# Fewer instructions on one to four numbers per partition, and another instruction order, in a one-core cross-attention and quantized-FFN kernel

## The chip, the cores and the metric

The kernel runs on one core of a Trainium2 chip. The metric is the device time of one execution in microseconds, as a median over runs. A separate profiled execution gives the instruction trace that the tables below are read from. The core has five engines that run side by side, each through its own instruction queue in order: PE (TensorE, matmuls), DVE (VectorE), ACT (ScalarE), POOL (GpSimd) and SP (SyncE, which here only issues DMAs).

## The reference: what is computed

Eight batches, each an input `x` of 256 rows by 512 columns and a second input (`media`) of the same size. Cut to what matters:

```
xn    = layernorm(x)
theta = theta_w . media + theta_b          phi = phi_w . xn + phi_b       g = g_w . xn + g_b
p     = softmax(theta^T phi)               t   = p g
h     = relu((t - mean(t)) * rsqrt(var(t) + 1e-5) * gamma + beta)      # mean over the whole batch
x     = x + tanh(g_xattn) * (out_w h + out_b + media)

y     = layernorm(x)
f     = silu(bitlinear(y, w1)) * bitlinear(y, w2)                       # 512 -> 2048
x     = x + tanh(g_ffn) * bitlinear(f, w3)                              # 2048 -> 512
```

`bitlinear` normalizes its input by its root mean square, quantizes each row to 8-bit levels by the row's largest magnitude, and quantizes the weights to -1, 0 and 1 by their mean magnitude. In the kernel, the quantized values are held as small integers in 16 or 8 bits and multiplied on PE; the scales come back afterwards as one number per row.

## The kernel before

**Tiles.** A row of `x` is a partition, so a batch is two tiles of 128 x 512 (index `c`). Attention works on batch `b`; the FFN works on row tiles `i = 2b + c`, sixteen in all, each with four groups `j` of 512 columns of `w1` (`ug`) and of `w2` (`uu`). Every PSUM tile is one of eight banks.

**Operations and their names.** The builder makes a list `OPS` of labelled operations, `name:b` or `name:i`. The ones that matter here:

- Layer norm of `x` (L344-355): `nb`, `na` statistics on DVE; `nr` adds the epsilon, `np` raises to -1/2 on POOL, `nm` negates the mean, `nx` applies both and writes `xn`.
- Projections and scores: `jtheta`, `jphi`, `jg` and `sm` on PE, `htheta`, `hphi`, `hg` copy them out of PSUM; `sx` takes the row maximum on DVE, `se` the exponential on ACT; `pd`, `pr`, `ph`, `pl` divide and split; `av` multiplies on PE.
- Norm over the batch (L560-593): `tx` copies the result, `tb`, `ta`, `tw` per-partition statistics, `tm` sums over partitions by a matmul with ones, `tu` divides by 128, `td` forms mean squared minus mean of squares, `tr` flips the sign and adds the epsilon, `tp` raises to -1/2 on POOL; `hc`, `hs`, `hr`, `hl` apply it.
- Out-projection and residual: `om` on PE, `oa` on DVE adds it to `x` and leaves each row's sum.
- FFN input (L635-684): `im` turns the row sum into minus the mean, once for each `c`; `iq` squares on ACT, `ir` takes the maximum on DVE, `iv`, `ie`, `ip`, `ic` make the scale, `iz` quantizes, `it` transposes by DMA. `ia`, `ib` form the row's scale, `if0` and `if1` multiply it by `w1`'s and `w2`'s factor (`back`, columns 0 and 1), `ig` takes the reciprocal (column 2).
- FFN tile `i` (L686-764): `us` (Silu, ACT, scaled by `back` column 0), `um` (product, DVE), `qs` sum of squares, `qa` row maximum, `qf` a floor for it out of `back` column 2, `qm`, `qc` the quantizing scale; `qe` an epsilon term out of `back` column 2, `qr`, `qp`, `qb` the factor for the way back; `qz` quantizes, `qt` transposes by DMA.
- Down-projection: `dm` and `da` plainly, or for batches 2 to 6 a seven-product scheme for 2 x 2 blocks (`tS` sums, `tP` products, `tU` and `tA` additions).
- Weights: `wl` loads a 1 MB chunk, `ws` sums magnitudes, `wr` and `wq` quantize; `wf` makes the factor of `w1` and `w2`.

**What sets the order.** Nothing is scheduled at run time. `CFG["order"]` (L68) is a written-out list of all 1512 operations; they are emitted in that order, and each engine executes its share in sequence. `CFG["alt"]` says for the operations that can run on several engines which one does. A small operation is declared by `tiny` (L162), which offers DVE (`v`) and POOL (`p`). All DMAs go through SP in the listed order, so one whose buffer isn't free holds the ones behind it. Work tiles come from pools: 31 buffers of 2 KB per partition, 7 of 4 KB, 7 of 8 KB; the weight chunks and the FFN's `h` share the last kind.

The small operations have the form

```python
def tiny(label, fn):
    op(label, v=lambda: fn(V), p=lambda: fn(G))
...
tiny(f"qf:{i}", lambda e_: e_.tensor_scalar(fl(), back()[:, c, 2:3], Q_EPS * RMS_EPS**0.5, 1.0, ALU.mult, ALU.mult))
```

Of the kernel before, what the change touches and what calls it, by code (L numbers as in the profile page):

```python
# [19 lines left out]
P = 128  # L20
# [69 lines left out]
def flamingo_gated_block(  # L90
# [86 lines left out]
    ones, neg_half = c_("ones", [P, P]), c_("neg_half", [P, 2 * DC])

    fac = {n: (c_(f"{n}_max", [P, DC]), c_(f"{n}_sum", [P, 1]), c_(f"{n}_back", [P, 1]), c_(f"{n}_fwd", [P, 1])) for n in ("phi", "g")}
    half_w = {n: c_(f"{n}_half", [P, 2, DC, L], F16) for n in ("phi", "g")}  # L180
    theta_hi, theta_lo = c_("theta_whi", [P, DC, L], F32R), c_("theta_wlo", [P, DC, L], F32R)
    cols2 = c_("cols2", [P, 2])
    bias = {"theta": (lambda: cols2()[:, 0:1]), "phi": (lambda: cols2()[:, 1:2])}

    whole_x = [b for b in range(B) if b not in CFG["xsplit"]]
    whole_m = [b for b in range(B) if b not in CFG["msplit"]]
    assert set(whole_x) <= set(whole_m)
    keep = {"phi": False, "g": any(b not in CFG["p32"] for b in whole_x), "theta": any(b not in whole_x for b in whole_m)}
    scaled_t = {n: c_(f"{n}_sc", [P, DC, L]) if k else w_(f"{n}_sc", [P, 2 * DC, L]) for n, k in keep.items()}
# [19 lines left out]
    def constants():  # L209
        op("C:ones", lambda: V.memset(ones(), 1.0))  # L210
        op("C:half", lambda: V.memset(neg_half(), -0.5))
        if CFG["p32"] or CFG["rpe"]:
            op("C:id0", lambda: G.memset(ident(), 0.0))
            op(
                "C:id1",
                lambda: G.affine_select(
                    out=ident(), in_=ident(), compare_op=ALU.not_equal, fill=1.0, base=0, pattern=[[-1, P]], channel_multiplier=1
                ),
            )
        wps = ps_("warm")  # L220

        op("C:warm", lambda: [PE.matmul(wps()[:, 0:P], ones(), ones(), start=True, stop=True) for _ in range(CFG["warm"])])
        for n in ("theta", "phi", "g"):
            load_proj(n)
        op("Lc:0", lambda: nc.sync.dma_start(out=cols(), in_=columns))
        op("Lgam:0", lambda: nc.sync.dma_start(out=gam(), in_=ln_gamma))
        op("Lbet:0", lambda: nc.sync.dma_start(out=bet(), in_=ln_beta))
        op("Low:0", lambda: nc.sync.dma_start(out=ow(), in_=out_wT))
        op("C:tanh", lambda: S.activation(tg(), gates(), AF.Tanh))
        if CFG["rpe"]:  # L230
            tiny("C:gid", lambda e: e.tensor_scalar(gident(), ident(), tg()[:, 0:1], 1.0, ALU.mult, ALU.mult))

        tiny("C:ow", lambda e: e.tensor_scalar(ow(), ow(), tg()[:, 0:1], 1.0, ALU.mult, ALU.mult))
        op("C:owh", a=lambda: S.copy(ow_hi(), ow()), v=lambda: V.tensor_copy(ow_hi(), ow()))
        tiny("C:owl", lambda e: e.tensor_tensor(ow_lo(), ow(), ow_hi().bitcast(F32), ALU.subtract))
        tiny("C:ob", lambda e: e.tensor_scalar(ob(), ob(), tg()[:, 0:1], 1.0, ALU.mult, ALU.mult))

        for n in ("phi", "g"):
            mx, sm, back, fwd = fac[n]
            tot = ps_(f"{n}_tot")
            op(f"C:{n}max", lambda n=n, mx=mx: V.tensor_reduce(mx(), proj_w[n](), AX.X, ALU.max, apply_absolute_value=True))
            op(f"C:{n}sum", lambda mx=mx, sm=sm: V.tensor_reduce(sm(), mx(), AX.X, ALU.add))
            op(f"C:{n}tot", lambda sm=sm, tot=tot: PE.matmul(tot()[:, 0:1], ones(), sm(), start=True, stop=True))
            lim = 1e-30 if n == "phi" else 1e-2
            op(f"C:{n}back", lambda tot=tot, back=back, lim=lim: V.tensor_scalar(back(), tot()[:, 0:1], lim, 1.0 / G_SCALE, ALU.max, ALU.mult))
            op(f"C:{n}fwd", lambda back=back, fwd=fwd: V.reciprocal(fwd(), back()))
            tiny(f"C:{n}w", lambda e, n=n, fwd=fwd: e.tensor_scalar(scaled_w[n](), proj_w[n](), fwd(), 1.0, ALU.mult, ALU.mult))  # L250
            op(
                f"C:{n}h",
                a=lambda n=n: S.copy(half_w[n]()[:, 0], scaled_w[n]()),
                v=lambda n=n: V.tensor_copy(half_w[n]()[:, 0], scaled_w[n]()),
            )
            tiny(f"C:{n}l", lambda e, n=n: e.tensor_tensor(half_w[n]()[:, 1], scaled_w[n](), half_w[n]()[:, 0], ALU.subtract))
        pback, pfwd = fac["phi"][2:]
        tiny("C:tw", lambda e: e.tensor_scalar(scaled_w["theta"](), proj_w["theta"](), pback(), 1.0, ALU.mult, ALU.mult))
        tiny("C:tb", lambda e: e.tensor_scalar(cols2()[:, 0:1], col["theta"](), pback(), 1.0, ALU.mult, ALU.mult))
        tiny("C:pb", lambda e: e.tensor_scalar(cols2()[:, 1:2], col["phi"](), pfwd(), 1.0, ALU.mult, ALU.mult))  # L260
        op(
            "C:th",
            a=lambda: S.copy(theta_hi(), scaled_w["theta"]()),
            v=lambda: V.tensor_copy(theta_hi(), scaled_w["theta"]()),
        )
        tiny("C:tl", lambda e: e.tensor_tensor(theta_lo(), scaled_w["theta"](), theta_hi().bitcast(F32), ALU.subtract))
        tiny("C:gback2", lambda e: e.tensor_scalar(gback(), fac["g"][2](), 1.0 / P_SCALE, 1.0, ALU.mult, ALU.mult))
# [4 lines left out]
    def weights(n):  # L272
# [30 lines left out]
        if n < 2:  # L303
            op(f"wf:{n}", lambda: V.tensor_scalar(wfac()[:, n : n + 1], wmean()[:, n : n + 1], 1.0 / (127.0 * Q_UNIT), None, ALU.mult))
        else:
            op(f"wf:{n}", lambda: V.tensor_scalar(wmean()[:, 2:3], wmean()[:, 2:3], tg()[:, 1:2], None, ALU.mult))
# [22 lines left out]
    def attention(b):  # L329
        xt, med = xs[b], meds[b]  # L330
        xsp, msp, osp = b in CFG["xsplit"], b in CFG["msplit"], b in CFG["osplit"]
        s32, p32 = b in CFG["s32"], b in CFG["p32"]

        w32 = {
            "phi": proj_w["phi"],
            "theta": scaled_w["theta"] if xsp else proj_w["theta"],
            "g": proj_w["g"] if p32 else scaled_w["g"],
        }
        bias_b = bias if xsp else col

        mv, rstd, nmu = s_("mv", f"mv{b}", [P, DC, 2]), s_("rstd", f"rstd{b}", DC), s_("nmu", f"nmu{b}", DC)
        xn = [w_(f"xn{b}_{c}", [P, T]) for c in range(DC)]
        for c in range(DC):
            st = s_("bst", f"bst{b}_{c}", V.BN_STATS_DIM)  # L344
            op(f"nb{c}:{b}", lambda c=c, st=st: V.bn_stats(st(), xt[c]()))  # L345
            op(f"na{c}:{b}", lambda c=c, st=st: V.bn_aggr(mv()[:, c, :], st()))
        tiny(f"nr:{b}", lambda e: e.tensor_scalar(rstd(), mv()[:, :, 1], LN_EPS, 1.0, ALU.add, ALU.mult))
        op(f"np:{b}", lambda: G.tensor_tensor(rstd(), rstd(), neg_half()[:, :DC], ALU.pow))
        tiny(f"nm:{b}", lambda e: e.tensor_scalar(nmu(), mv()[:, :, 0], -1.0, 1.0, ALU.mult, ALU.mult))

        def norm(eng, c):
            return eng.tensor_scalar(xn[c](), xt[c](), nmu()[:, c : c + 1], rstd()[:, c : c + 1], ALU.add, ALU.mult)

# [240 lines left out]
        else:  # L594
# [4 lines left out]
                p=lambda: G.tensor_scalar(h(), h(), 3e38, 0.0, ALU.min, ALU.max),  # L599
            )  # L600

        osums = sums[b] = []
        for c in range(DC):
            o = ps_(f"o_ps{b}_{c}")

# [28 lines left out]
    def ffn_in(b):  # L634
# [10 lines left out]

        for c in range(DC):
            sq = w_(f"fsq{b}_{c}", [P, T])  # L650
            tiny(f"im{c}:{b}", lambda e, c=c: e.tensor_scalar(nmu()[:, c : c + 1], sums[b][c](), -1.0 / T, 1.0, ALU.mult, ALU.mult))  # L651
# [308 lines left out]
```

## Time and profile before

| what | value |
|---|---|
| median of 3 runs | 280.13 us (279.75 to 280.41) |
| profiled execution: device time | 279.37 us |
| profiled execution: span of the trace | 277.6 us |
| instructions on DVE, ACT, POOL | 537, 337, 273 |
| granted clock of PE | 0.999 |
| first real matmul | 6.47 us |
| last matmul ends | 274.38 us |

The profile's groups give, for each source line and shape, how many instructions ran, how long the engine was busy with them, the mean of one, and how long the engine had idled just before them. The timeline lists instructions by start, with the idle time before one and what ended it in brackets. The chain of waits goes back from the end: at each step to what released an instruction, or to its predecessor on the engine.

### The profile page before, as it was taken

How to read it: one execution, taken by the hardware profiler on the slowest of the kernel's cores; microseconds unless marked ns; L12 is line 12 of the kernel's file. 1: busy time of each engine (PE TensorE's matmuls, PEld its weight loads, DVE VectorE, ACT ScalarE, POOL GpSimd, SP SyncE). 2: the span in 40 equal slices, each digit the busy share in tenths (PEclk: the TensorE clock that was granted, in tenths of full speed). 3: DMA queues.
4: the chain of work that ended last, by engine and by line, in shares of the span. 5: the costliest groups of instructions: out<-in, count | busy, mean ns of one | idle time of the engine just before them, and what ended most of it. 6: DMA issues, size and time to landing. Idle time of an engine off the chain costs nothing.

```text
span 277.6 us, 4741 instructions
## 1 busy us (share of the span) xinstructions
PE 271.3 (98%) x1574; PEld 166.9 (60%) x1574; DVE 254.0 (91%) x537; ACT 227.6 (82%) x337; POOL 205.9 (74%) x273
## 2 busy tenths in 40 slices
PE   7999999999899999999999999999999999999995
PEld 7458585564365555545754778655545566457863
DVE  3798988999999989989999899997999889999895
ACT  1399999999989999899999899895867789675910
POOL 2588774799999998867896989758785855873461
PEclk9999999999999999999999999999999999999999
DMA  7999979998761325134948815916372356605685
GB/s 217 357 347 374 387 277 367 184 195 327 154 115 38 79 41 110 40 76 130 155 97 180 161 41 113 154 34 118 88 142 76 61 130 113 151 2 110 77 211 212
DMA packets 81528, 43.30 MB, mean 156 GB/s; under 512 B 67936, under 2 KB 69088, under 8 KB 81504
## 3 DMA queue, kind: packets, MB, share of 16 engines
q1 hardware_dynamic: 81504, 43.00, 62.2%
q8 instruction: 12, 0.20, 0.3%
q14 instruction: 12, 0.10, 0.1%
HBM read 22.02 MB, written 4.19 MB: 94 GB/s over the span
## 4 chain that ended last, share of the span: by engine, by line
PE 82%; DVE 8%; ACT 3%; issue 2%; DMA 2%; POOL 1%; SPq 0%; POOLq 0%; ACTq 0%
PE fup L699 18%; PE fgp L699 17%; PE dp L857 10%; PE fop L772 6%; PE av L538 4%; PE sc L463 4%; PE phi_ps L385 4%; PE theta_ps L385 3%; PE gx_ps L416 3%; PE tp L498 3%; PE o_ps L610 3%; PE sc L461 3%; PE av L551 3%; DVE nmax L472 2%; DMA med<-in_media 2%
## 5 line engine op out<-in xcount | busy, mean ns | idle before, releaser
L699 PEld LDWEIGHTS <-fqt 128*128 128x128 f16 x512 | 49.0, 99 | 56.8 <-issue 3.2
L699 PE MATMUL fgp<-w1q,fqt 128*128 128x512 f16 x256 | 61.7, 379 | 1.4 <-ACT fh L709 1.4
L699 PE MATMUL fup<-w2q,fqt 128*128 128x512 f16 x256 | 62.3, 379 | 0.0
L709 ACT ACTIVATE fh<-fgp,fback 128x512 f32<-128x512 f32 x64 | 41.1, 687 | 10.4 <-PE fgp L699 8.9
L711 DVE TENSOR_TENSOR fh<-fup,fh 128x512 f32<-128x512 f32 x64 | 42.6, 681 | 2.8 <-PE fup L699 1.6
L732 DVE TENSOR_REDUCE fham<-fh 128x1 f32<-128x2048 f32 x15 | 34.2, 2280 | 0.1
L731 ACT ACTIVATE fhq<-fh 128x2048 bf16<-128x2048 f32 x15 | 28.7, 1913 | 0.4 <-POOL fhfl L733 0.4
L745 ACT ACTIVATE fhq<-fh,fhqs 128x2048 f16<-128x2048 f32 (+1 forms) x14 | 26.6, 1907 | 1.9 <-DVE fhqs L735 1.7
L475 ACT ACTIVATE e<-sc,nmax 128x512 f32<-128x512 f32 x32 | 21.8, 689 | 2.8 <-DVE nmax L472 2.3
L772 PE MATMUL fop<-w3q,fhi 128*128 128x512 fp8e4 (+1 forms) x112 | 22.9, 349 | 0.0
L472 DVE TENSOR_REDUCE nmax<-sc 128x1 f32<-128x512 f32 x32 | 21.6, 681 | 0.7 <-PE sc L463 0.3
L450 POOL TENSOR_TENSOR x<-x,med 128x512 f32<-128x512 f32 x14 | 19.3, 1375 | 3.8 <-ACT med L444 3.7
L519 DVE SCALAR_TENSOR_TENSOR ph<-e,rden,ph 128x512 f16<-128x512 f32 x24 | 17.8, 760 | 0.0
L857 PEld LDWEIGHTS <-fhi 128*128 128x128 f16 x160 | 15.6, 98 | 3.6
L538 PE MATMUL av<-pt,gx 128*128 128x256 f16 x144 | 17.5, 273 | 0.0
L772 PEld LDWEIGHTS <-fhi 128*128 128x128 f16 x112 | 10.6, 98 | 9.3 <-DMA fhi<-fhq 0.4
L538 PEld LDWEIGHTS <-gx 128*128 128x128 f16 x144 | 13.8, 98 | 3.4 <-issue 0.3
L667 POOL TENSOR_SCALAR fq<-x,fnmu,fqs 128x512 f16<-128x512 f32 x16 | 14.1, 889 | 0.8 <-DVE fqs L663 0.2
L654 ACT ACTIVATE fsq<-x,fnmu 128x512 f32<-128x512 f32 x16 | 11.5, 719 | 3.1 <-DVE fnmu L651 2.3
L345 DVE BATCH_NORM_STATS2 bst<-x 128x6 f32<-128x512 f32 x16 | 10.8, 683 | 3.3 <-DMA x<-in_x 3.2
L416 PEld LDWEIGHTS <-xh 128*128 128x128 f16 x144 | 9.4, 98 | 5.5 <-issue 3.3
L621 DVE SCALAR_TENSOR_TENSOR x<-o_ps,x 128x512 f32<-128x512 f32 x16 | 10.9, 687 | 1.9 <-PE o_ps L610 1.6
(223 smaller groups left out, 688.9 us busy)
## 6 DMA issues: line engine op xcount, KB each, us to landing
x<-in_x SPq DMA_DIRECT2D x16, 256.0 KB, 4.0
med<-in_media SPq DMA_DIRECT2D x16, 256.0 KB, 4.5
w<-in_w2T SPq DMA_DIRECT2D x4, 1024.0 KB, 7.7
w<-in_w1T SPq DMA_DIRECT2D x4, 1024.0 KB, 8.2
w<-in_w3T SPq DMA_DIRECT2D x4, 1024.0 KB, 9.7
out<-x SPq DMA_DIRECT2D x15, 256.0 KB, 2.3
fhi<-fhq SPq DMA_TRANSPOSE x17, 4.4
gam<-in_ln_gamma SPq DMA_DIRECT2D x1, 256.0 KB, 10.4
```

The costliest lines, as they stand in the source:

```text
L385: PE.matmul(ps(), w, v, start=c == 0 and k == 0, stop=c == DC - 1 and k == e)
L472: op(f"sx{t}:{b}", lambda sc=sc, nmax=nmax: V.tensor_reduce(nmax(), sc(), AX.X, ALU.max, negate=True))
L475: lambda t=t, sc=sc, nmax=nmax, e=e: S.activation(e(), sc(), AF.Exp, bias=nmax(), accum_out=den()[:, t : t + 1]),
L538: PE.matmul(av()[:, ts(g, TG * P)], gx()[:, hg, ts(s, L)], v[:, hp, s], start=k == 0, stop=k == 3 * TCH - 1)
L699: PE.matmul(ps(), qt()[:, c * EC + k, :], wq[n][j]()[:, k, :], start=k == 0, stop=k == EC - 1)
L709: lambda j=j, gp=gp: S.activation(h()[:, ts(j, 512)], gp(), AF.Silu, scale=back()[:, c, 0:1]),
L711: op(f"um{j}:{i}", lambda j=j, up=up: V.tensor_tensor(h()[:, ts(j, 512)], up(), h()[:, ts(j, 512)], ALU.mult))
L731: op(f"qs:{i}", lambda: S.activation(hq().bitcast(BF16), h(), AF.Square, accum_out=ss()[:, 0:1]))
L732: op(f"qa:{i}", lambda: V.tensor_reduce(am()[:, 0:1], h(), AX.X, ALU.max, apply_absolute_value=True))
L745: return S.mul(hq()[:, sl], h()[:, sl], qs())
L772: PE.matmul(o()[:, sl], hi()[:, f, :], wq[2][f // 4]()[:, f % 4, sl], start=f == 0, stop=f == FC - 1)
L857: PE.matmul(banks[n]()[:, h * HT : (h + 1) * HT], l()[:, f, :], r(f), start=f == 0, stop=f == HC - 1)
```

## The change

54 instructions fewer (1512 operations become 1458): 64 go and 10 come.

- `nm` goes (8): `nx` subtracts the mean where it added the negated one.
- `tr` goes (8): the epsilon is added in `tu`, by a constant tile `eps2` with 0 and 1e-5, and `td` subtracts the other way round, so that `tp` can take its result. Two memsets (`C:e0`, `C:e1`) fill `eps2`.
- `im` is done once for both `c` (8 fewer); the two row sums now lie in one tile.
- `if0` and `if1` become one `if` that multiplies by both factors at once (8 fewer), with both inputs broadcast.
- `qf` goes (16): its constant is taken into `w2`'s factor in `wf`, so that the reciprocal in `back` column 2 is the floor.
- `qe` goes (16): a new `ge` (8, on DVE) writes the epsilon term for both `c` into `back` column 3.

Beside that, the lists of engines and of the order are replaced as a whole. Of the operations kept, 40 go from POOL to DVE, 39 from DVE to POOL, 11 from ACT to POOL, 12 from POOL to ACT, 9 from ACT to DVE and 3 from DVE to ACT. The matmuls are the same ones in another order, as are the 105 DMA issues. The order of the first DMAs, for example:

```
before  Lx0:0 Lx1:0 LWtheta Lm0:0 Lm1:0 Lc LWphi Lm0:1 Lx1:1 Lx0:1 Lx0:3 Lm1:1 LWg Low ... wl1:0 wl3:0 wl0:0 Lgam wl2:0 Lbet Lm0:3 wl0:2
after   Lx0:0 Lx1:0 Lm0:0 LWtheta Lm1:0 LWphi LWg Lc Lx0:1 Lx1:1 Lx0:2 Lx1:2 Low ... wl3:0 wl1:0 Lbet wl0:0 Lgam wl0:2 wl2:0 Lm1:5
```

and DVE's order from batch 0's residual sums to the factor that its first Silu reads:

```
before  oa1:0 oa0:0 hs:1 pl3:2 ir1:0 ir0:0 pl2:2 ie:0 ltheta:3 lphi:3 wm:0 lg:2 wn:0 wc:0 oa0:1 oa1:1 sx1:3 im1:1 sx0:3
        lg:3 sx2:3 wq2:0 wq3:0 sx3:3 wf:0 wf:1 ir0:1 ir1:1 wq2:1 iv:1 wq3:1 if0:0
after   oa0:0 oa1:0 hs:1 wm:0 pl2:2 ir1:0 ir0:0 wn:0 ie:0 wc:0 lg:2 lphi:3 ic:0 ltheta:3 lg:3 oa0:1 wq2:0 oa1:1 im:1 wq3:0
        sx2:3 wq0:1 sx0:3 sx3:3 ir0:1 ir1:1 iv:1 sx1:3 ia:0 ie:1 wf:0 ib:0 tb:2 wq2:1 if:0
```

The diff of the code, without the two long lists:

```diff
+    eps2 = c_("eps2", [P, 2])
+    op("C:e0", lambda: G.memset(eps2(), 0.0))
+    op("C:e1", lambda: G.memset(eps2()[:, 1:2], LN_EPS))
...
-            op(f"wf:{n}", ... wmean()[:, n : n + 1], 1.0 / (127.0 * Q_UNIT), None, ALU.mult)
+            unit = 1.0 / (127.0 * Q_UNIT) / (Q_EPS * RMS_EPS**0.5 if n else 1.0)
+            op(f"wf:{n}", ... wmean()[:, n : n + 1], unit, None, ALU.mult)
...
-        tiny(f"nm:{b}", lambda e: e.tensor_scalar(nmu(), mv()[:, :, 0], -1.0, 1.0, ALU.mult, ALU.mult))
-            return eng.tensor_scalar(xn[c](), xt[c](), nmu()[:, c : c + 1], rstd()[:, c : c + 1], ALU.add, ALU.mult)
+            return eng.tensor_scalar(xn[c](), xt[c](), mv()[:, c, 0:1], rstd()[:, c : c + 1], ALU.subtract, ALU.mult)
...
-        op(f"tu:{b}", lambda: V.tensor_scalar(mu(), mps()[:, 0:2], 1.0 / P, None, ALU.mult))
+        op(f"tu:{b}", lambda: V.scalar_tensor_tensor(mu(), mps()[:, 0:2], 1.0 / P, eps2(), ALU.mult, ALU.add))
-            lambda: V.scalar_tensor_tensor(var(), mu()[:, 0:1], mu()[:, 0:1], mu()[:, 1:2], ALU.mult, ALU.subtract),
+            lambda: V.scalar_tensor_tensor(
+                var(), mu()[:, 0:1], mu()[:, 0:1], mu()[:, 1:2], ALU.mult, ALU.subtract, reverse1=True
+            ),
-        tiny(f"tr:{b}", lambda e: e.tensor_scalar(rs(), var(), -1.0, LN_EPS, ALU.mult, ALU.add))
-        op(f"tp:{b}", lambda: G.tensor_tensor(rs(), rs(), neg_half()[:, 0:1], ALU.pow))
+        op(f"tp:{b}", lambda: G.tensor_tensor(rs(), var(), neg_half()[:, 0:1], ALU.pow))
...
+        tiny(f"im:{b}", lambda e: e.tensor_scalar(nmu(), sums[b](), -1.0 / T, 1.0, ALU.mult, ALU.mult))
-            tiny(f"im{c}:{b}", lambda e, c=c: e.tensor_scalar(nmu()[:, c : c + 1], sums[b][c](), -1.0 / T, 1.0, ALU.mult, ALU.mult))
...
-        for k in range(2):
-            tiny(f"if{k}:{b}", lambda e, k=k: e.tensor_scalar(back()[:, :, k], am(), wfac()[:, k : k + 1], 1.0, ALU.mult, ALU.mult))
+        tiny(f"if:{b}", lambda e: e.tensor_tensor(back()[:, :, 0:2], am().unsqueeze(2).to_broadcast([P, DC, 2]),
+                                                  wfac().unsqueeze(1).to_broadcast([P, DC, 2]), ALU.mult))
+        op(f"ge:{b}", lambda: V.scalar_tensor_tensor(back()[:, :, 3], back()[:, :, 2], 1.0 / Q_EPS**2, back()[:, :, 2], ALU.mult, ALU.mult))
...
-        tiny(f"qf:{i}", lambda e_: e_.tensor_scalar(fl(), back()[:, c, 2:3], Q_EPS * RMS_EPS**0.5, 1.0, ALU.mult, ALU.mult))
-        op(f"qm:{i}", lambda: V.tensor_scalar(am()[:, 0:1], am()[:, 0:1], fl(), 1.0 / (127.0 * Q_UNIT), ALU.max, ALU.mult))
+        op(f"qm:{i}", lambda: V.tensor_scalar(am()[:, 0:1], am()[:, 0:1], back()[:, c, 2:3], 1.0 / (127.0 * Q_UNIT), ALU.max, ALU.mult))
-        tiny(f"qe:{i}", lambda e_: e_.tensor_scalar(e(), back()[:, c, 2:3], back()[:, c, 2:3], RMS_EPS, ALU.mult, ALU.mult))
-        tiny(f"qr:{i}", lambda e_: e_.tensor_scalar(r(), ss()[:, 0:1], 1.0 / FF, e(), ALU.mult, ALU.add))
+        tiny(f"qr:{i}", lambda e_: e_.tensor_scalar(r(), ss()[:, 0:1], 1.0 / FF, back()[:, c, 3:4], ALU.mult, ALU.add))
```

## The prediction

> **What bounds the kernel now.** I read the page's engine line first, then the groups by line with shapes kept apart, the timeline of TensorE, the chain of waits inside 40 to 80 us, and last the timeline of 57 to 77 us.
>
> From the page:
>
> ```profile
> PE 271.3 (98%) x1574; PEld 166.9 (60%) x1574; DVE 254.0 (91%) x537; ACT 227.6 (82%) x337; POOL 205.9 (74%) x273
> ```
>
> TensorE is idle for 6.3 us of 277.6: 1.04 before its warm-up matmuls, 0.62 before the first real one at 6.47 us, 1.35 at 73 us, and 3.18 after its last one ended at 274.38 (the last DVE addition at 274.42 and its store). "Busy" could hide waiting, so I checked spacing: twenty FFN matmuls of 512 columns in a row take 4.32 us in the chain, 216 ns each, and nearly every FFN group in the timeline keeps that. Adding the excess over each kind's usual spacing gives 2.3 us between 6.47 and 274.38, of which 1.5 at 71.3 us, and nothing else above 0.3. So about 265.6 us is matmul work that no order of the other engines can shorten. The Trainium skill (Perfetto Trace Analysis, "Identifying the Most-Contended Engine") distrusts matmul occupancy and would judge headroom by LDWEIGHTS busy time: 60% here, which would leave some 110 us. The 216 ns spacing contradicts that in this trace, and the sum below does not use it.
>
> What ends the one real wait, in the chain of 40 to 80 us (start, duration, what):
>
> ```profile
> 48.93 0.04 DVE x L621
> ...
> 58.78 1.21 DVE w1q L321 x2
> ...
> 62.49 1.15 DVE fz L659
> 63.65 0.59 DVE w2q L321
> 64.24 0.16 DVE fback L680
> ...
> 64.47 1.28 ACT L709
> ...
> 68.22 1.89 ACT wj L296 x2
> ...
> 71.14 1.86 ACT fh L709 x3
> 73.03 1.90 PE fgp L699 x8
> ```
>
> From 48.9 to 64.4 the chain is DVE's own queue: statistics of batches 0 and 1, W1/W2 quantization and the maxima of batch 3, back to back until if0:0 (L680) writes the scale that the first Silu needs. Then it is ACT's queue, a table load first. The timeline of the same place:
>
> ```profile
> 62.41 1.24 DVE L659 TENSOR_SCALAR fz<-fz 128x2 f32<-128x2 f32 x1
> ...
> 72.10 1.22 DVE L676 TENSOR_TENSOR fam<-fam,fr 128x2 f32<-128x2 f32 x1
> ...
> 73.02 4.00 PEld L699 LDWEIGHTS <-fqt 128*128 128x128 f16 x20 [1.84 <-DMA fqt<-fq]
> 73.03 1.90 PE L699 MATMUL fgp<-w1q,fqt 128*128 128x512 f16 x8 [1.35 <-ACT fh L709]
> ```
>
> Two things came late together: a PSUM bank (Silu at 73.0) and batch 1's transposed input, issued at 69.69, landed at 72.98. And two-number instructions took 1.2 us here.
>
> **What the algebra removes.** Rows by shape, count by mean: nm (L349) 5x162 ns DVE, 3x192 POOL; tr (L577) 2x138, 6x473; im (L651) 8x147, 8x317; if (L680) 7x319, 9x475; qf (L733) 4x138, 12x193; qe (L737) 5x199, 11x472. That is 6.0 us of DVE and 17.7 of POOL. Coming back: im as one instruction (2 DVE, 6 POOL: 0.3 and 1.9), if as one TENSOR_TENSOR on four numbers (2 DVE, 6 POOL), ge eight times on DVE (nearest row L661, the same kind on two numbers, 212 ns: 1.7), two memsets (rows 99 to 205 ns: 0.2 on POOL). The merged if is not in the trace: between 149 ns (fastest DVE L675) and 1.35 us (slowest POOL L680); I take the means of L676, 552 and 456 ns (its kind, scalars aside): 1.1 and 2.7. Net: DVE -2.9, POOL -12.9.
>
> Here a rule speaks against the merged if and the extra DVE work: the Trainium skill (SBUF — State Buffer, "Who interferes with whom") says that a DVE instruction with two SBUF inputs and a POOL one that reads SBUF exclude each other for a whole instruction. By it every if and ia on DVE beside a POOL addition could cost up to that addition's 1.4 us. The fz row above fits in size, though with one tensor input; the sum uses the row means, which hold such collisions already.
>
> **What the new sequence spends.** 114 kept operations change engine. Adding each queue in its new order, each instruction at the median start-to-start time of its row: DVE 247.4 before, 249.3 after; ACT 217.0 and 211.7; POOL 188.3 and 181.9. So DVE's relief is spent on full-width work taken from ACT and POOL (hr and hg of batches 0 and 7 and tx of 7, for instance). TensorE has the same 1467 matmul calls: nothing gained in work. What can change is waits, at three places.
>
> *Start.* Lm0:0 moves ahead of LWtheta on SP. The issues stood at 2.11 and 1.65 with 4.22 to landing for med; at 1.65 it lands near 5.9, and warm-up ends at 5.85. theta_w, now second, also lands near 5.9 (3.8 after issue). The first matmul gains up to 0.5. Behind it C:gtot waits for g_w (13th on SP, now 7th, so near 3.5 + 3.8 to 5.2 = 7.3 to 8.7) and on DVE for gmax, phimax, phisum, nb0:1, gsum (0.41+0.41+0.15+0.69+0.15 = 1.8): ready at 9.1 to 10.5, while TensorE comes at about 9.6. Bounds -0.5 to +0.5; I take -0.3. nx0:0 moves to POOL (0.85 against 0.54) and is hidden by four theta matmuls (1.8 us).
>
> *48 to 78 us.* Batch 1's last out-projection to its first FFN group: 18.0 us of TensorE work lay between, now 19.4. On POOL, ip:1 comes behind iz1:0 by rx0, wr0, rm1, wr1, rx1 (1.4+2.2+1.0+2.2+1.4 = 8.2 us; before 9.6 from 55.90 to 65.54); with iz1:0 at about 56.2 to 57.0, ip:1 starts at 64.4 to 65.2, and by the old steps (ip 1.5, np 1.2, ic 0.4, two iz 2.0, transposition 3.3) it lands at 72.8 to 73.6, against a need near 73.7. So the 1.35 goes, just. What is late next is PSUM. DVE's queue from the later residual sum of batch 0 to if:0 is 14.7 us against 14.3, and that sum comes 0.3 later: if:0 ends near 65.1, and table load and Silu (1.28+0.69) free the first bank at 67.1, while TensorE, with eight tiles out since 59.8, wants the ninth at 66.8. Then ACT runs four Silus, |w3| sums (2.1 us) and only two more Silus before ph and another 2.1 us, so the seventh Silu ends near 77; TensorE's 18th tile is due at 74.5 and depends on um3:1, near 75.1. I count 0.3 + 0.5 = 0.8 of new waiting; bounds 0 (other banks are free) and 2.5 (the seventh Silu's bank is the one assigned). Net -1.35 + 0.8 = -0.55.
>
> W1's last chunk (wl2:0) now goes to SP behind a W3 chunk; both need a freed 8 KB buffer. 1 MB more ahead of it at some 360 GB/s (slices 2 to 5 of the page) is 2.9 us: landing 41.85 becomes 44.7. Its reader ws2:0 ran at 47.8; 3 us cover it, and each microsecond beyond would delay all of W1.
>
> *Rest.* At the later stage marks (out-projections, first FFN groups, down-projections of batches 2 to 7) TensorE's work in front agrees within 2 us in most cases, and up to 10 in a few that are not waited for; DVE's work in front of batches' statistics differs by -2.4 to +3.6 us while it idles 23.6 in all. Merging im makes batch b's first squares wait for both residual sums (0.7); 11.7 us or more lie between out-projection and FFN, so it costs nothing unless that cover shrinks. ge stands late (for batch 7 behind qz1) and is read only by qr, off the path. At the end, the tile order is nearly the same; from um0:14 at 255.0 DVE has 19.5 us queued, ending near 274.5 to 275.1 against 274.9 before: +0.1, bounds 0 and +0.5.
>
> **Sum.** -0.3 -0.55 +0.1 = -0.75 us. The profiled execution was 279.37 (span 277.6 and 1.8 around it), giving 278.6; the shown median is 280.13, 0.76 above it, so I forecast 279.4. A floor: all 0.62 + 1.35 and the small gaps gone is 277.4 by the median.
>
> **The rivals.**
>
> A, the wait only moves. For it: batch 1's landing clears by 0.1 us at best in the late case, and the same eight banks remain. Against: ip:1's queue is 1.4 us shorter. New waits equal to the old 1.5 leave only the start: 280.0.
>
> B, slower: the scale at if:0. It stands behind ia:0, ib:0, tb:2, wq2:1 on DVE, and ia:0, ib:0 were on POOL before. If two of these meet POOL's additions as L659 and L676 did (1.24 and 1.22 instead of 0.16 and 0.28: +2.0), the first Silu frees a bank 2.3 us after TensorE needs it, and the sparse Silus behind |w3| add the upper bound's other 1.6. That is 3.9 instead of 0.8, less gains: 280.13 - 0.3 - 1.35 + 3.9 + 0.1 = 282.5. It decides from if:0 later than about 66.4. For it: DVE is full there. Against: POOL has fewer instructions to collide with.
>
> C, slower elsewhere: another stage's late input, as hr:1 before the batch-1 out-projection (POOL's queue in front of it grew from 32.4 to 33.5, its slack was 0.7) or W1's chunk: +0.5 to +2, 280.8 to 282.
>
> **Numbers.** Forecast case 277.6 to 279.5: 0.5. A, 279.6 to 280.7: 0.2. B 0.18, C 0.12: together slower, 0.3. The range 277.6 to 282.5 leaves out the ends of B and a better start. 0.2% (0.56 us) is about what a measurement of this kernel tells from no change.
>
> **What would show it.** Right: first real matmul near 6.1; no TensorE gap above 1 us at 71 to 78; DVE busy within 3 us of 254, POOL down by 10. Wrong: if:0 after 66.4, a gap at the ninth FFN tile, C:gtot waiting, or a tail beyond 3.2 us after the last matmul. Gaps of over 1 us in batches 2 to 7 would refute the reading that the rest is unchanged.

## The result and the profile after

| | median | range | runs |
|---|---|---|---|
| before | 279.94 us | 278.88 to 280.41 | 4 |
| after | 288.13 us | 287.88 to 288.29 | 4 |

The ratio is 1.0297, with an interval of 1.0266 to 1.0329: the change costs 8.2 us. The forecast was 279.4, and the range ended at 282.5.

The page of the changed kernel has this engine line (busy time, share of the span, instructions), to be held against the one in the prediction:

```profile
PE 273.1 (95%) x1574; PEld 166.5 (58%) x1574; DVE 257.3 (90%) x525; ACT 222.3 (78%) x332; POOL 209.9 (73%) x234
```

TensorE runs the same 1574 matmuls in a longer span, 286.5 us against 277.6. GpSimd has 39 instructions fewer and is busy 4.0 us longer, where the prediction had it down by 10 or more. With each matmul's usual spacing taken off, much as in the prediction, TensorE waits about 12.1 us between its first real matmul and its last, against about 2.5 before (the prediction counted 2.3; the split depends by some tenths on which matmuls are taken as one kind). That is 9.6 us more; the first real matmul comes 0.3 earlier (6.15), the spacing itself sums to 0.4 less (265.0 against 265.4), the tail after the last matmul is the same (3.20): 8.9 in all, the growth of the span.

The waits stand in the timeline of TensorE after the change (start, duration, line, tile; in brackets the idle time before and what ended it):

```profile
8.50 1.98 PE L388 MATMUL phi_ps<-xn,phi_w 128*128 128x512 f32 x4 [0.40 <-POOL xn L355]
27.38 0.71 PE L501 MATMUL tp<-dg,e 128*128 128x128 f32 x4 [1.02 <-POOL dg L491]
33.79 0.49 PE L501 MATMUL tp<-dg,e 128*128 128x128 f32 x2 [1.76 <-POOL dg L491]
70.39 1.90 PE L712 MATMUL fup<-w2q,fqt 128*128 128x512 f16 x8 [1.75 <-DVE w2q L325]
72.54 1.02 PE L712 MATMUL fgp<-w1q,fqt 128*128 128x512 f16 x4 [0.25 <-ACT fh L722]
80.25 1.02 PE L712 MATMUL fup<-w2q,fqt 128*128 128x512 f16 x4 [1.96 <-DVE fh L724]
102.64 4.49 PE L712 MATMUL fgp<-w1q,fqt 128*128 128x512 f16 x20 [0.67 <-DMA fqt<-fq]
167.66 0.45 PE L419 MATMUL gx_ps<-g_half,xh 128*128 128x128 f16 x5 [1.36 <-POOL xh L363]
```

Two kinds matter. Four waits end on GpSimd, three before 34 us and one at 167.7, together 4.5 us, at places where the kernel before had none as long. Those at 70 and 80 us end on VectorE, together 3.7; before, there was one of 1.35 us at 73.0.

Why GpSimd is late shows in the groups of the normalization `nx`, which writes `xn` (times are min/median/max in ns, then from when to when). Before:

```profile
L352 POOL TENSOR_SCALAR xn<-x,nmu,rstd x12: 759/770/1292, 13.1 to 154.3; 128x512 f32<-128x512 f32 x12
```

After, for GpSimd and for VectorE:

```profile
L355 POOL TENSOR_SCALAR xn<-x,mv,rstd x12: 2072/2086/2505, 6.1 to 163.3; 128x512 f32<-128x512 f32 x12
L355 DVE TENSOR_SCALAR xn<-x,mv,rstd x4: 540/546/547, 6.0 to 122.7; 128x512 f32<-128x512 f32 x4
```

Same shape, same types, same two numbers per partition; add and multiply became subtract and multiply. On VectorE nothing happens (540 ns before). On GpSimd one instruction goes from 0.77 us to 2.09, and twelve of them cost 16.2 us more by their means (2200 against 849 ns). GpSimd's timeline around the second wait shows how that reaches TensorE:

```profile
28.88 0.38 POOL L491 TENSOR_SCALAR dg<-ident,rden 128x128 f32<-128x128 f32 x1
29.25 4.14 POOL L355 TENSOR_SCALAR xn<-x,mv,rstd 128x512 f32<-128x512 f32 x2
33.37 0.37 POOL L491 TENSOR_SCALAR dg<-ident,rden 128x128 f32<-128x128 f32 x1
```

Two normalizations for a later batch stand in the queue between two 0.4 us steps that TensorE needs at once. The second `dg` ends at 33.74, and TensorE's transposition starts at 33.79. The wait at 167.7 is of the same kind: two normalizations of 4.15 us in all stand on GpSimd ahead of the step `xh` that TensorE waits for.

### The profile page after: what moved, and what is told of

Same layout as the page of the kernel before. It is cut to its first block, busy times and chain, and to the rows that moved or that the text cites. A ratio compares the mean times of both kernels' runs of the same rounds, so it can differ in the third digit from the quotient of the medians.

```text
span 286.5 us, 4676 instructions
## 1 busy us (share of the span) xinstructions
PE 273.1 (95%) x1574; PEld 166.5 (58%) x1574; DVE 257.3 (90%) x525; ACT 222.3 (78%) x332; POOL 209.9 (73%) x234
## 4 chain that ended last, share of the span: by engine, by line
PE 71%; DVE 10%; POOL 3%; issue 2%; DMA 1%; ACT 1%; ACTq 0%; POOLq 0%; DVEq 0%
PE fup L712 16%; PE fgp L712 16%; PE dp L870 11%; PE fop L783 7%; PE sc L466 4%; PE av L541 4%; PE o_ps L614 3%; PE av L554 2%; PE gx_ps L419 2%; PE phi_ps L388 2%; PE theta_ps L388 2%; DMA fqt<-fq 1%; POOL xn L355 1%; DVE fz L658 1%; PE tp L501 1%
## 5 line engine op out<-in xcount | busy, mean ns | idle before, releaser
L722 ACT ACTIVATE fh<-fgp,fback 128x512 f32<-128x512 f32 x64 | 41.7, 689 | 13.1 <-PE fgp L712 11.7
L355 POOL TENSOR_SCALAR xn<-x,mv,rstd 128x512 f32<-128x512 f32 x12 | 26.4, 2200 | 1.2 <-PE gx_ps L419 0.6
L756 ACT ACTIVATE fhq<-fh,fhqs 128x2048 f16<-128x2048 f32 (+1 forms) x12 | 22.7, 1893 | 0.0
L453 POOL TENSOR_TENSOR x<-x,med 128x512 f32<-128x512 f32 x14 | 17.9, 1278 | 0.1
L664 POOL TENSOR_TENSOR fr<-fz,neg_half 128x4 f32<-128x4 f32 x8 | 9.2, 1153 | 8.1 <-DVE fz L663 4.9
L669 POOL TENSOR_SCALAR fq<-x,fnmu,fqs 128x512 f16<-128x512 f32 x16 | 13.0, 820 | 1.5 <-DVE fqs L665 1.0
```

The source lines that it names most:

```text
L355: return eng.tensor_scalar(xn[c](), xt[c](), mv()[:, c, 0:1], rstd()[:, c : c + 1], ALU.subtract, ALU.mult)
L722: lambda j=j, gp=gp: S.activation(h()[:, ts(j, 512)], gp(), AF.Silu, scale=back()[:, c, 0:1]),
L756: return S.mul(hq()[:, sl], h()[:, sl], qs())
```

## The experiments

Theory Q: two causes add up, the operation pair of `nx` on GpSimd, and the new order, which puts what TensorE needs between 60 and 80 us too late on VectorE; the rest of the algebra is nearly harmless. Rivals: the stride of the mean that `nx` now reads (P), the other pieces of the algebra (E, later R), or the scale at `if:0` (the prediction's rival B). Each time stands against runs of the kernel before on the same chip (279.4 to 279.8 us).

| run | what it is | median us | ratio and interval |
|---|---|---|---|
| e1_add | after, `nx` adds in place of subtracting | 283.39 | 1.0134 (1.0107 to 1.0161) |
| e2_nm | after, `nx` as before, `nm` back on VectorE | 283.19 | 1.0138 (1.0123 to 1.0153) |
| e3_before_sub | before, `nx` as after | 286.04 | 1.0248 (1.0230 to 1.0266) |
| e5_forms | e2_nm, eight forms of `nx` | 286.23 | one run |
| e4_algebra_old_order | old order, new algebra but `nx` | 286.64 | 1.0255 (1.0240 to 1.0271) |
| e9_algebra_no_im | the same, `im` as before | 280.71 | 1.0033 (1.0021 to 1.0045) |
| e15_im1_on_vector | e4, `im:1` moved | 285.23 | 1.0201 (1.0174 to 1.0228) |
| e14_order_alone | new order, old algebra | 283.74 | 1.0155 (1.0133 to 1.0176) |
| e6_scale_early | e2, `if:0` early, `wq2:1` early | 282.17 | 1.0102 (1.0072 to 1.0132) |
| e10_product_early | e6, `um3:1` early | 281.76 | 1.0076 (1.0057 to 1.0095) |
| e11_two_means | e10, `im` split again | 282.05 | 1.0082 (1.0067 to 1.0097) |
| e8_before_scale_early | before, `if0:0` early | 279.51 | 0.9994 (0.9982 to 1.0006) |
| e12_before_batch1_early | before, batch 1's chain early | 279.41 | 0.9991 (0.9981 to 1.0000) |
| e13_no_im_batch1_early | e9, the same | 281.23 | 1.0067 (1.0048 to 1.0085) |

### The normalization's operations: e1_add, e2_nm, e3_before_sub, e5_forms

The edit of e1_add, in the changed kernel:

```
-            return eng.tensor_scalar(xn[c](), xt[c](), mv()[:, c, 0:1], rstd()[:, c : c + 1], ALU.subtract, ALU.mult)
+            return eng.tensor_scalar(xn[c](), xt[c](), mv()[:, c, 0:1], rstd()[:, c : c + 1], ALU.add, ALU.mult)
```

> The changed kernel with one word altered: nx adds the mean where it should subtract it (so the normalized x is off by twice the mean over the deviation); same instructions, engines, order and operands. Theory S (the operation subtract in a two-scalar instruction on POOL is slow, 2.1 us for 128x512 where add then multiply takes 0.77): the 12 POOL nx fall to about 0.8 us each, POOL loses some 16 us, the TensorE gaps at 26, 32, 68 and 78 us go or shrink, and the time is 279 to 281. Rival P (slow because the scalar is now read with a stride out of the statistics tile): nx stays at 2.1 us, time within 1 of 288.1. Rival O (the sequence is poor whatever nx costs): nx falls but the time stays above 285.

The edit of e2_nm, in the changed kernel (the negation stands behind `nr`, on VectorE):

```
+                V.tensor_scalar(nmu(), mv()[:, :, 0], -1.0, 1.0, ALU.mult, ALU.mult),
...
-            return eng.tensor_scalar(xn[c](), xt[c](), mv()[:, c, 0:1], rstd()[:, c : c + 1], ALU.subtract, ALU.mult)
+            return eng.tensor_scalar(xn[c](), xt[c](), nmu()[:, c : c + 1], rstd()[:, c : c + 1], ALU.add, ALU.mult)
```

> The changed kernel with nm given back: eight small DVE instructions at the place of nr in the order, and nx adds the dense negated mean as before; all else of the change stays. S: nx 0.8 us on POOL, time 279 to 281.5 (eight DVE instructions of some 70 ns each). P: the same, 279 to 281.5, since the scalar is dense again. O: above 285.

The edit of e3_before_sub, in the kernel before:

```
-        tiny(f"nm:{b}", lambda e: e.tensor_scalar(nmu(), mv()[:, :, 0], -1.0, 1.0, ALU.mult, ALU.mult))
...
-            return eng.tensor_scalar(xn[c](), xt[c](), nmu()[:, c : c + 1], rstd()[:, c : c + 1], ALU.add, ALU.mult)
+            return eng.tensor_scalar(xn[c](), xt[c](), mv()[:, c, 0:1], rstd()[:, c : c + 1], ALU.subtract, ALU.mult)
```

> The kernel before, its own order and engines, with only the nx edit of the change: nm emits nothing and nx subtracts the mean out of the statistics tile. S and P: the 12 nx that stand on POOL here take 2.1 us each instead of 0.85, some 15 us more on POOL, and the time rises by 3 to 10, to 283 to 290. O (nx is not the cause): within 1 of 280.

Measured: 283.39, 283.19 and 286.04. The first two lie above theory S's ranges and below rival O's: `nx` is a cause, but not the only one. The groups of `xn` on GpSimd, in e1_add, where only the operation differs from the changed kernel:

```profile
L355 POOL TENSOR_SCALAR xn<-x,mv,rstd x12: 757/767/1193, 6.3 to 158.7; 128x512 f32<-128x512 f32 x12
```

and in e3_before_sub, where the old order meets the new pair:

```profile
L352 POOL TENSOR_SCALAR xn<-x,mv,rstd x12: 2063/2074/2519, 12.6 to 159.5; 128x512 f32<-128x512 f32 x12
```

The duration follows the operation, in both orders, with the strided mean in both. The one edit alone makes the kernel before 6.7 us slower. In the new order it accounts for 4.4 of the 8.2 us (8.2 less e2_nm's 3.8, each against its own runs of before), and 3.8 stay. None of the four waits that ended on GpSimd is left in e2_nm's timeline of TensorE; those for VectorE near 70 and 80 us are.

e5_forms gives each batch its own form:

```
+            form = {
+                0: (ALU.subtract, ALU.mult), 1: (ALU.add, ALU.mult), 2: (ALU.subtract, ALU.mult), 3: (ALU.mult, ALU.subtract),
+                4: (ALU.subtract, ALU.subtract), 5: (ALU.add, ALU.add), 6: (ALU.max, ALU.mult), 7: (ALU.mult, ALU.add),
+            }[b]
+            shift = nmu()[:, c : c + 1] if b == 2 else mv()[:, c, 0:1]
+            return eng.tensor_scalar(xn[c](), xt[c](), shift, rstd()[:, c : c + 1], *form)
```

> The changed kernel with nm given back, and nx with another pair of operations in each batch, so that one profile shows the cost of each form on POOL (the values from nx on are not the reference's): batch 0 subtract, multiply with the strided mean; 1 add, multiply with the strided mean; 2 subtract, multiply with the dense negated mean; 3 multiply, subtract; 4 subtract, subtract; 5 add, add; 6 max, multiply; 7 multiply, add. S: 2.1 us wherever subtract stands (batches 0, 2, 3, 4), about 0.77 in 1, 5 and 7, and open for max. P: 2.1 us in all but batch 2, whose scalar is dense, and 0.77 there. The time is of no interest.

GpSimd's timeline of it; the lines belong to batches 1, 2, 3, 4, 5, 6 and 7:

```profile
12.95 0.77 POOL L366 TENSOR_SCALAR xn<-x,mv,rstd 128x512 f32<-128x512 f32 x1
15.66 2.35 POOL L366 TENSOR_SCALAR xn<-x,nmu,rstd 128x512 f32<-128x512 f32 x1
27.98 4.14 POOL L366 TENSOR_SCALAR xn<-x,mv,rstd 128x512 f32<-128x512 f32 x2
...
77.08 2.50 POOL L366 TENSOR_SCALAR xn<-x,mv,rstd 128x512 f32<-128x512 f32 x1
106.20 2.08 POOL L366 TENSOR_SCALAR xn<-x,mv,rstd 128x512 f32<-128x512 f32 x1
132.99 2.08 POOL L366 TENSOR_SCALAR xn<-x,mv,rstd 128x512 f32<-128x512 f32 x1
...
160.43 1.53 POOL L366 TENSOR_SCALAR xn<-x,mv,rstd 128x512 f32<-128x512 f32 x2 [0.74 <-PE gx_ps L430]
```

The second line is the decisive one: a dense mean with subtract and multiply takes 2.35 us, as much as the strided one of batch 0, so the stride (rival P) is not it. Add then multiply takes 0.77, multiply then add 0.77 each; multiply then subtract 2.07, add then add 2.08, maximum then multiply 2.08. So it isn't the subtraction as such, as theory S had it: adding twice is as slow, and of the pairs tried only those of one addition and one multiplication are fast. Subtracting twice took 2.50 and 2.51, but that is of the place and not of the pair, for in the changed kernel subtract and multiply take as long for the same batch:

```profile
73.64 2.50 POOL L355 TENSOR_SCALAR xn<-x,mv,rstd 128x512 f32<-128x512 f32 x1
```

The 2.35 of batches 0 and 2 stand in the changed kernel too (2.35 each), where other batches take 2.07. VectorE ran three of the pairs (subtract and multiply, add and multiply, add twice) and took 0.53 to 0.55 for each.

### Order and algebra apart: e4, e9, e15, e14

e4_algebra_old_order takes e2_nm's code and lists its steps in the order and on the engines of the kernel before; `im` stands where the first of `im0` and `im1` stood, or behind the later residual sum.

> All of the algebra except nx (nm and the addition kept), in the order and on the engines of the kernel before: tr, qf, qe dropped, if in the place of the first of the two, im in the place of the old ones, ge behind ig. Theory Q (what is left after nx, 3.8 us, is the new sequence's queue on DVE between 50 and 78 us): 278.5 to 280, level with the kernel before or a little faster, 46 instructions fewer. Rival E (the new forms themselves cost: the broadcast if, ge, im for both row tiles): 281.5 to 284.

Measured 286.64, above what either theory gave, so something in the algebra did cost there. The longest waits of TensorE in e4 are two for the FFN's transposed input, of batch 0 (landed at 61.93) and of batch 1 (landed at 75.85); for the first the timeline names an exponential on ACT, but the matmul starts right behind the landing:

```profile
61.97 1.90 PE L713 MATMUL fup<-w2q,fqt 128*128 128x512 f16 x8 [1.50 <-ACT e L479]
75.90 1.90 PE L713 MATMUL fgp<-w1q,fqt 128*128 128x512 f16 x8 [1.76 <-DMA fqt<-fq]
```

GpSimd's timeline in e4 (`fnmu` is `im:1`, `fq` is `iz0:0` and `iz1:0`):

```profile
54.81 0.19 POOL L666 TENSOR_SCALAR fqs<-fr 128x2 f32<-128x2 f32 x1
57.15 0.19 POOL L652 TENSOR_SCALAR fnmu<-osum 128x2 f32<-128x2 f32 x1 [2.15 <-DVE x L624]
57.33 1.53 POOL L670 TENSOR_SCALAR fq<-x,fnmu,fqs 128x512 f16<-128x512 f32 x2
```

The merged `im:1` waits for batch 1's second residual sum, and the quantization of batch 0 queues behind it. Two runs test this. e9_algebra_no_im has e4's code and order with one edit (`im0`, `im1` and `iq0:3`, which need not wait for the second sum now, stand at their places of the kernel before):

```
-        tiny(f"im:{b}", lambda e: e.tensor_scalar(nmu(), sums[b](), -1.0 / T, 1.0, ALU.mult, ALU.mult))
...
+            tiny(f"im{c}:{b}", lambda e, c=c: e.tensor_scalar(nmu()[:, c : c + 1], sums[b]()[:, c : c + 1], -1.0 / T, 1.0, ALU.mult, ALU.mult))
```

> The order and the engines of the kernel before; of the algebra all but two pieces: the normalisation keeps the negated mean (nm, add and mult), and the negated mean of the channel sums stays two instructions (im0, im1, each at its old place on its old engine). So tr, qf and qe are gone, tu, td and qr take over their constants, if is one instruction on two factors, ge is new. Theory Q (the algebra itself is harmless; what made the order of before slow with it was the merged im, which must wait for the second residual sum): 278.3 to 280.2, the waits of TensorE at 60.2 (uu1:0, 1.66) and at 111.7 (sm1:4, 1.3) gone. Rival R (an order written out for 1512 steps is upset by any step that goes, whichever it is): 281.5 to 287, with waits of TensorE of over 1 us at other places.

e15_im1_on_vector is e4 with one step moved:

```
 order  ... oa1:1 -> im:1 -> sx1:3 ...        (e4: ... oa1:1 -> sx1:3 -> im:1 ...)
 "im:1": "p"  ->  VectorE
```

> The run called e4_algebra_old_order with one step moved: the merged im of batch 1 stands on VectorE right behind oa1:1 in place of GpSimd ahead of iz0:0. If its wait on GpSimd (2.15 us at 57.15) is what made uu1:0 late: iz0:0 starts near 55 in place of 57.33, the wait of 1.66 us at 60.2 goes, and the time falls from 286.6 to 283.5 to 285.3. If not: 286 to 287.2.

Measured: e9 280.71, half a microsecond above its range's end and far below rival R's; e15 285.23. So in the old order, at the places that e4 gives it, the merged `im` costs 5.9 us (286.64 less 280.71), and all the other algebra 0.9 by its ratio. Moving `im:1` off GpSimd returns 1.4: `iz0:0` starts at 55.42 in place of 57.33, the wait before 61.97 is gone and the one for batch 1's input falls from 1.76 to 0.36, but one of 1.39 appears two tiles later, in e15's timeline of TensorE:

```profile
63.91 2.76 PE L713 MATMUL fgp<-w1q,fqt 128*128 128x512 f16 x12 [1.39 <-DVE w1q L325]
```

A second place is batch 3: with two means, `iq0:3` ran at 103.25 in e9, ahead of the second residual sum (104.59). Merged, it waits for that sum and for an `im:3` that took 1.30 us on VectorE, and runs at 108.65 in e15 and 109.75 in e4; both lose 1.3 us before `sm1:4` there. How the remaining microseconds divide among the later batches was not taken apart.

e14_order_alone is the other half: all 54 instructions restored, in the new order.

```
 order  of the changed kernel, with nm behind nr, tr ahead of tp, im -> im0 im1, if -> if0 if1,
        qf and qe some 12 steps ahead of qm and qr
        (im0, im1, if0 and if1 on the engine of the merged step, which for 13 of the 32 is another than before)
```

> All 54 instructions restored, in the new order and on the new engines: nm behind nr, tr ahead of tp, im0 and im1 at the place of im, if0 and if1 at the place of if, qf and qe some 12 steps ahead of qm and qr and behind ig, each on the engine that it had before. Theory Q (the new order carries what is left, the algebra is close to harmless): 283 to 285.5, at or above the 283.2 of the run called e2_nm, with waits of over 1 us between 60 and 80 us. Rival R (the pieces of algebra cost by themselves): 280 to 281.8.

Measured 283.74, a ratio of 1.0155 (1.0133 to 1.0176), beside 1.0138 (1.0123 to 1.0153) for e2_nm: the order alone costs what e2_nm costs. TensorE's timeline has the same two waits, in e14_order_alone

```profile
66.77 1.90 PE L699 MATMUL fup<-w2q,fqt 128*128 128x512 f16 x8 [1.67 <-DVE w2q L321]
...
76.43 1.02 PE L699 MATMUL fup<-w2q,fqt 128*128 128x512 f16 x4 [1.96 <-DVE fh L711]
```

and in e2_nm

```profile
67.32 1.90 PE L718 MATMUL fup<-w2q,fqt 128*128 128x512 f16 x8 [1.74 <-DVE w2q L325]
...
76.87 1.02 PE L718 MATMUL fup<-w2q,fqt 128*128 128x512 f16 x4 [1.65 <-DVE fh L730]
```

The rest of the loss belongs to the order, and the algebra (without `nx`) is worth at most some tenths of a microsecond in it.

### What in the order: e6, e10, e11

In e2_nm the chain of waits from 46 to 80 us runs on VectorE without a break from 53.3 to 67.3 (start, duration):

```profile
63.30 1.19 DVE fz L664 x2
64.49 0.72 DVE fz L667
65.20 0.59 DVE nmax L481
65.86 0.07 DVE fz L669
66.07 0.60 DVE tst L574
66.67 0.59 DVE w2q L325
67.26 0.08 DVE fback L687
```

The last two lines are `wq2:1`, for which TensorE waits, and behind it `if:0`, for which the first Silu waits: at 67.3, past the 66.4 from which rival B should decide. e6_scale_early moves both on VectorE:

```
 order  ... ic:0 wf:0 wf:1 ia:0 ib:0 if:0 ...        (e2_nm: further down)
        wq2:1 and wq0:1 change places
```

> The changed kernel with nm given back (283.2), and two edits of its order only: wf:0, wf:1, ia:0, ib:0 and if:0 directly behind ic:0 instead of ten DVE instructions later, and wq2:1 and wq0:1 exchanged. Q: the TensorE gap of 1.9 us in front of uu2:0 goes, the first Silu comes about 1 us earlier (ACT's exponentials are then in front of it), and of the 4.1 us of gaps between 64 and 77 us 2 to 3 go: 280.2 to 281.4. Rival E, or a sequence that is late in many places: the gaps come back further on, 282.6 to 283.6.

Measured 282.17, between the two. The wait for `wq2:1` is gone, and yet only about 1 us comes back, because `uu3:0` still waits 2.0 for `um3:1`. The early scale gains little for the first Silu: `if:0` now runs at 54.9 in place of 67.2, but the first Silu at 67.43 in place of 68.73, since four exponentials stand ahead of it on ACT, the last of which starts at 65.34 after 1.35 us of waiting for VectorE. e10_product_early moves the product too:

```
 order  ... uu3:1 um3:1 ge:0 tu:2 ia:1 pl2:3 ib:1 hc:2 td:2 if:1 ...        (e6: um3:1 behind if:1)
```

> The new order with the negated mean, the scale of batch 0 early (the run called e6_scale_early), and one more step moved: the 18th gated product (um3:1) stands on VectorE right behind pl3:3, ahead of ge:0, tu:2, ia:1, pl2:3, ib:1, hc:2, td:2 and if:1, some 2.9 us earlier than at 74.94. Theory Q (what is left of the loss is the order on VectorE between 60 and 78 us): the wait of 2.14 us before uu3:0 falls under 0.4 and the time falls from 282.2 to 279.9 to 280.9. Rival S (the steps it is moved past are as late as it is, and the wait moves to the next tile that needs them): 281.6 to 282.6, with a new wait of over 1 us between 74 and 85.

Measured 281.76: within rival S's range, not theory Q's. The wait at `uu3:0` is gone, and in TensorE's timeline of e10 this one has come up, with 78.6 in place of 75.7:

```profile
68.19 1.02 PE L718 MATMUL fgp<-w1q,fqt 128*128 128x512 f16 x4 [0.82 <-ACT fh L728]
78.61 1.02 PE L718 MATMUL fgp<-w1q,fqt 128*128 128x512 f16 x4 [1.30 <-DVE fh L730]
```

It is for `um3:0`, which VectorE starts at 77.88, as in e6 (77.80): that product didn't come later, TensorE now comes to it sooner. VectorE is busy 23.8 of the 24 us from 58 to 82 in this run, and just as long in the kernel before. So its load alone doesn't make an order slow there; what counts is which products stand early, and mending one uncovers the next.

e11_two_means asks whether the merged `im` costs in this order too:

```
-        tiny(f"im:{b}", lambda e: e.tensor_scalar(nmu(), sums[b](), -1.0 / T, 1.0, ALU.mult, ALU.mult))
...
+            tiny(f"im{c}:{b}", lambda e, c=c: e.tensor_scalar(nmu()[:, c : c + 1], sums[b]()[:, c : c + 1], -1.0 / T, 1.0, ALU.mult, ALU.mult))
 order  ... oa0 im0 ... oa1 im1 ...
```

> The run called e10_product_early with the merged im split again: im0 and im1 are two instructions, on VectorE right behind their residual sums in batches 1 to 5 and 7, both on GpSimd at the place of im in batches 0 and 6. Theory M (the merged im, which waits for the second residual sum and took 1.22 us in batch 1, carries part of what is left in the new order too): iq0:1 starts 1 us earlier and iq0:2 0.7 us earlier, and the time falls from 281.8 to 280.0 to 281.2. Theory O (what is left is the order on VectorE alone): 281.3 to 282.4, the waits before ug0:1 (1.0 at 67.0), ug1:3 (1.5 at 76.9) and ug3:5 (1.1 at 96.5) as they were.

Measured 282.05, no better: `iq0:1` did start earlier (59.30 against 59.82), but of the three waits two stayed and only the last fell, from 1.1 to 0.4. In the new order the merged `im` costs nothing that can be measured, as the prediction said; theory M fell. A new wait of 0.3 stands at 116 us.

### What sets the wait of the kernel before: e8, e12, e13

The kernel before has one long wait, 1.35 us at 73 us; the prediction named two things that came late together there, a PSUM bank and batch 1's transposed input. e8_before_scale_early was to free the banks earlier:

```
 order  ... ib:0 wf:0 wf:1 if0:0 ...        (before: if0:0 behind wq3:1; ib:0 now ahead of wr0:0)
```

> The kernel before with if0:0 moved in its order from behind wq3:1 to directly behind wf:1 (ib:0 in front of wr0:0 on POOL for that): the first Silu comes some 3 us earlier. If the PSUM banks set the gap of 1.35 us at 71 us there, it shrinks: 278.2 to 279.0. If the transposed input of batch 1 sets it (landed at 72.98), the time stays within 0.4 of 279.4.

Measured 279.51, no change, and the wait is still there. But it says nothing of the banks: `if0:0` ended at 62.26 in place of 64.39, while the first Silu started at 65.59, hardly earlier than the 65.76 before, again behind ACT's exponentials and the table load. What the run does show is that the wait ends with the input, as in the kernel before (landed at 73.30, against 72.98):

```profile
73.35 2.70 PEld L699 LDWEIGHTS <-fqt 128*128 128x128 f16 x14 [1.85 <-DMA fqt<-fq]
```

e12_before_batch1_early brings the input:

```
 order  DVE   ir1:1 iv:1 ie:1 wq2:1 ...
        POOL  rx0:2 ip:1 ic:1 iz0:1 iz1:1 rm1:3 np:4 ...
```

> The kernel before with the chain of batch 1 from its sums to its quantized input earlier: on VectorE iv:1 and ie:1 ahead of wq2:1 and wq3:1, on GpSimd ip:1, ic:1, iz0:1 and iz1:1 ahead of rm1:3 and np:4. Theory T (the one long wait of the kernel before, 1.51 us at 71.3 before ug1:3, is for the transposed input of batch 1): iz1:1 ends near 67.5 in place of 69.67, the wait goes and the time falls from 279.7 to 278.0 to 278.9. Rival V (VectorE is full there, and the tiles that need its products wait in its place): 279.2 to 280.2, with a wait of over 1 us between 66 and 82 at another tile.

`iz1:1` ended at 68.18 (before: 69.67), and two short waits took the long one's place:

```profile
68.74 0.35 PE L571 MATMUL mu_ps<-mv,ones 128*128 128x2 f32 x2 [0.15 <-DVE mv L569]
70.29 1.89 PE L699 MATMUL fgp<-w1q,fqt 128*128 128x512 f16 x8 [0.31 <-DVE fh L711]
```

The time, 279.41, is 0.9991 of before with an interval that ends at 1.0000: a few tenths of a microsecond, hardly more than nothing. That is rival V's range, though not its sign, for no wait of over 1 us came up. The input was the late one: `ug1:3`, the tile that waited, starts 0.05 us after the input lands in all three runs (72.98 and 73.03 before, 73.30 and 73.35 in e8, here 72.91 and 72.96).

```profile
72.96 1.41 PEld L699 LDWEIGHTS <-fqt 128*128 128x128 f16 x8 [0.42 <-DMA fqt<-fq]
```

The Silu that ended at 73.0 in the kernel before was not what it waited for: in the list that Silu stands behind `ug1:3`, and in e12 it ends at 74.35, when the tile has long begun. What the moves could gain was small, since the transposition, issued 1.5 us earlier, took 4.7 us to land in place of 3.3. What an input that lands early would be worth is not shown. The same moves in e9's code:

> The same two moves in the run called e9_algebra_no_im (the old order with the algebra except the normalisation and the merged im). By theory T its waits at 68.1 and 72.1 (0.61 and 0.65) go: 279.2 to 280.1, from 280.7. By rival V 280.3 to 281.3.

Measured 281.23, 0.5 slower than e9_algebra_no_im, within rival V's range. No version was found that is clearly faster than the kernel before.

## Why the prediction was wrong

**The step that failed first is the cost of the algebra.** "What the algebra removes" counted the instructions that go and come, and left out the one that stays and is altered: `nx` with subtract for add. Where it does speak of `nx` ("nx0:0 moves to POOL (0.85 against 0.54) and is hidden") it uses the old form's row for the new form. That row doesn't show the new operation; its cost had to be bounded from both sides, as the prediction did for the merged `if`. Its median was 2.09 us, twelve times, and 4.4 of the 8.2 us hang on it (e2_nm). The terms that were counted came out near: from e14_order_alone to e2_nm, which differ in the algebra without `nx`, GpSimd's busy time falls by 13.3 us (12.9 forecast) and VectorE's by 0.8 (2.9 forecast; since e2_nm keeps all eight `nm`, and on VectorE, 1.6 of that was to be expected here).

**The second is the size of the new waiting between 48 and 78 us.** The prediction had 0.8 us with an upper bound of 2.5. In e2_nm the excess over usual spacing is 1.9 us before `uu2:0`, 0.4 before `ug0:1` and 1.8 before `uu3:0`: 4.1. The place and one mechanism were right, since a tile (`uu3:0`, the fifteenth of the FFN in the list) does wait for `um3:1`, as the prediction had it for its 18th; the product came at 76.8 in place of 75.1. The other was not seen: `uu2:0` needs `wq2:1`, a weight chunk on VectorE. The prediction asked there for PSUM banks and for the scale alone, although it named `wq2:1` among the steps ahead of `if:0`. Its reading of the old wait, a bank and an input late together, was right for the input alone (e8, e12).

**Rival B** had the direction, and for the part without `nx` nearly the price: 282.5, with e2_nm at 283.2 and `if:0` ended at 67.3. That is mostly luck. Its 3.9 us were to be banks freed late by the Silus, and only the 0.4 before `ug0:1` ended on one; the rest waited for `wq2:1` and `um3:1`. With `if:0` at 54.9 and `wq2:1` mended as well, 2.6 of 3.8 us stayed (e6_scale_early, against its own runs of before).

**Right:** that the 265 us of matmul work don't change (265.0); the first real matmul near 6.1 (6.15, in part luck, since the profiles of the other runs in the new order have it anywhere from 5.9 to 7.2); the tail of 3.2; that the order spends VectorE's relief: against before, the order alone raises its busy time by 4.5 us (258.5 in e14_order_alone), where the prediction's sums give 4.8, and ACT's falls by 5.2 (5.3 forecast). The old wait at 71 to 73 us did go. That merging `im` costs nothing held for the new order (e11_two_means); in the old order it costs 5.9 us at the places that e4 gives it, part of it because it stands on GpSimd ahead of the quantization of batch 0. The signs against the forecast that came true were `if:0` after 66.4, GpSimd up by 4 where 10 less was the sign, and VectorE at 257.3, just outside the 3 us around 254. GpSimd's sign failed by `nx` alone: with an addition in its place it is busy 193.1 us in e1_add, 12.8 less than before. Of rival C's two places the W1 chunk is no cause: it landed at 44.2 in e2_nm, where 44.7 was forecast, and no wait for it shows.

**Open:** the 2.1 us that remain in e10_product_early. The waits that its trace shows are at `sm0:3` (0.6), `ug0:1` (1.0), `ug1:3` (1.5) and `ug3:5` (1.1), three of the four ended by VectorE. Each move made there uncovered a further wait, and no run took them away together.

## What to carry to other kernels

An instruction that stays but changes its operation is a new instruction: look for a row with exactly that operation on that engine, and where there is none, bound it, on GpSimd above all, where the pair of operations alone took the time from 0.77 to 2.09 us. An algebraic saving of small instructions off the critical path is worth what the path sees of it, here some tenths of a microsecond; merging two of them makes the earlier wait for the later, and can cost microseconds where the merged one stands in a queue ahead of something urgent. In a stage where one engine is full, compare orders by what each tile of the bound engine needs, weights included, not by the sum of a queue. And where two events end within 0.05 us of each other, the profile's name for what ended a wait can be the wrong one: the list of steps tells which of them the instruction can wait for at all.

## What the runs showed of the hardware

- GpSimd's TENSOR_SCALAR with two per-partition numbers on 128x512 float32 takes 0.77 us for add then multiply and multiply then add, and some 2.07 us for four other pairs, subtract and multiply among them, which reaches 2.35 and 2.5 at some places of the program (after, e5_forms); subtract twice ran only at the places of 2.5. VectorE takes 0.53 to 0.55 for the three pairs that it ran (e5_forms).
- The fast time fits the Trainium skill (GPSIMD Engine Reference, "3.1 Elementwise — side-by-side cycle accounting"), which gives a best case of 1.8 cycles per element and 769 ns for 512 elements.
- VectorE's `im` on two numbers, 0.17 to 0.24 us elsewhere, took 1.22 (`im:1` in e10_product_early) and 1.30 (`im:3` in e15_im1_on_vector). What they met there was not isolated.
- A DMA transposition that took 3.3 us from issue to landing in the kernel before took 4.7 when it was issued 1.5 us earlier (batch 1's input in e12_before_batch1_early).
